# Weight blocks, first queries by halves, the order of the end, and 24 products into an unused bank, in a two-layer gated cross-attention kernel

## The chip, the cores and the metric

The kernel runs on one core of one Trainium2 chip. The metric is the device time of one launch in microseconds (us). The kernel before took 1123.73 us, the median of three runs (1122.61 to 1124.41). Its page and trace come from one profiled execution of 1121.98 us.

A core has five engines, each working through its own queue in order: TensorE (PE; its weight loads are listed apart as PEld), VectorE (DVE), ScalarE (ACT), GpSimd (POOL) and SyncE (SP, which here only issues transfers). An engine waits at an instruction until what it needs has been signalled by another engine or a transfer; everything behind it on that engine waits too.

## What is computed

Four batches `x` of 512 tokens by 512 features go through two layers, each a cross attention and a feed-forward block, both with gates:

```python
x = x + tanh(g_xattn[0]) * L0_xattn(layernorm(x), ctx)      # a WKV recurrence
x = x + tanh(g_ffn[0])   * L0_ffn(layernorm(x), w1, w2, w3)  # 1-bit weights
x = x + tanh(g_xattn[1]) * L1_xattn(layernorm(x), ctx, wq, bq, wkv, bkv, wp, bp)
x = x + tanh(g_ffn[1])   * L1_ffn(layernorm(x), gamma, W)
```

The change touches only layer 1 and its weights:

- `L1_xattn` is attention with 16 heads of 32. The rows of x and of the output, and the weights `wq` and `wp`, are rounded to 8-bit integers: `s = max(absmax(row) / 127, 1e-8)`, `round(x / s)` clipped to ±127, and the products are scaled back by both s.
- `L1_ffn` is one product. Each row is normalised by its root mean square, multiplied by gamma and rounded to 8 bits by its absmax; the weight W is rounded to −1, 0 or 1 after division by its mean absolute value.

## The kernel before, in words

**Tiles.** Batch b lives in `xb`, 128 partitions by 4 row tiles by 512 features; "row t" below is a tile of 128 tokens. A product of depth 512 is four matmuls over blocks of 128. Integer operands are bf16, others f32.

**The order.** Instruction order is laid out by hand. Each stage is a generator, called a line; `place` gives each of its steps a place in time, counted in batches of 17 slots (SLOTS), one slot being about one unit of the attention or of the feed-forward. `run` always advances the line with the lowest place, and the steps' matmuls are chained in the order in which they were emitted (`next_turn`). An `event` is a line of one step (L1332 to L1340). The other engines get what the steps emit; a scheduler keeps each engine's queue near that order. In the boot phase, which lasts until layer 0's feed-forward of batch 0 has ended, places are given by `at_us` or `at_unit`, and there are two PSUM banks with tag m for everything that is not a long sum; later there are three of m, three of hp and two of acc.

**Weights (boot).** `wq`, `wp` and W (keys q, p, f) are loaded as 128x2048 tiles `wn` by `load`. `rounded` (L407) takes the absmax of a whole weight in one DVE reduction (output `w_am`), the scales (`int8_scale`), and then three DVE steps (`quantise`, L253 to L255) for each of four 128x512 blocks into the bf16 `wi` (tag sg, two buffers). For W, `ternary_sums` (L421, output `w_part`) and `ternary` (L430) do the same with one mean. `ints_turned` (L444) transposes the blocks on PE into a bank (`wt_ps`) and DVE copies them (L336) into wqT, wpT or wfT. `output_scales` (L448) transposes wp's scales (`pb_ps`); DVE multiplies them by the gate into `swp_b`. Beside all this run batch 0's feed-forward (`ff_z`, `hr`), the keys and values of the context (`k_half`, V from `v_ps`) and batch 1's WKV recurrence (`wk_q`).

**Attention of layer 1 (`attention_layer`, L855).** `prepared` rounds a row of x and transposes it (`qr_ps`). `project(g)` (L901) makes the queries of four heads for all rows, splits them into two f32r parts (`at_half`) and writes them to memory (`qD`); `fetch_queries` (L939) reads them back, repeated over partitions, as `at_qR`, 4 transfers for a unit (two heads, two rows). SP issues writes and reads in one queue. A unit: `scores` (`s_ps`, maximum on DVE, exponential on ACT), then `turned` (four transposes into `pt_ps`, copied by ACT or DVE), `values` (`o_ps`) and `collect`. There are 16 units a batch, each stage one unit behind the other. The last batch (`alone`) has no feed-forward left beside it; instead batch 2's `ternary_layer` is spread over its units.

**The end.** `project_out` rounds a row of the attention's output, transposes it (`at_oqT`), multiplies it by wpT (`p_ps`) and adds it to x. `statistics` (L1130) gives mean and inverse root of rows; the inverse root is computed by DVE (`rsqrt`, L182: shift, guess, three Newton rounds of three small steps), or by POOL but for its first two steps (`rsqrt_aside`, L199). `ternary` (L1147) makes `tf_xn`, its absmax and scales (`tf_s`, L1162 to L1176), rounds on ACT (L264), transposes (`qr_ps`, ACT's L271 into `tf_xT`), multiplies by wfT (`f_ps`), and DVE's L1189 adds the product to x, which is then stored. For the last batch `end` (L1072) does rows 0 and 1 together, then rows 2 and 3, one step behind the first two; the rsqrt of rows 2 and 3 is POOL's.

Of the kernel before, what the change touches and what calls it, by code (L numbers as in the profile page):

```python
# [30 lines left out]
def kernel(  # L31
# [42 lines left out]
    QSCALE = 1.0 / math.sqrt(DH)  # L74
    GS = 64
    ROWS = 3
    NG = D // GS

    cp = ctx.enter_context(tc.tile_pool(name="const", bufs=1))
# [229 lines left out]
    class Weights:  # L309
# [97 lines left out]
        def rounded(self, key):  # L407
            wn = self.raw.pop(key)
            am = sm.tile([P, NC], F32, name="w_am", tag="w_am")
            absmax(am, wn)  # L410
            s = sq if key == "q" else self.sp
            r = sm.tile([P, NC], F32, name="w_r", tag="w_r")
            int8_scale(s, r, am)
            wi = self.pool.tile([P, NC, D], BF16, name="wi", tag="sg", bufs=2)
            for j in range(NC):
                quantise(wi[:, j, :], wn[:, j, :], r[:, j : j + 1], -127.0)
            self.ints[key] = wi
            if key == "q":
                nc.vector.tensor_scalar(sq, sq, QSCALE, None, ALU.mult)

# [9 lines left out]
        def ternary(self):  # L430
            wn = self.raw.pop("f")
            mf = self.mean_abs(self.fsum, D * D)
            nc.vector.tensor_scalar(mf, mf, 1e-5, None, ALU.add)
            nc.vector.tensor_scalar(
                coef[:, 3:4], mf, gates[:, 3:4], 1.0 / 127.0, ALU.mult, ALU.mult
            )
            rf = cp.tile([P, 1], F32, name="rf")
            nc.vector.reciprocal(rf, mf)
            wi = self.pool.tile([P, NC, D], BF16, name="wi", tag="sg", bufs=2)
            for j in range(NC):  # L440
                quantise(wi[:, j, :], wn[:, j, :], rf, -1.0, 1.0)
            self.ints["f"] = wi

        def ints_turned(self, key):  # L444
            dst = {"q": wqT, "p": wpT, "f": wfT}[key]
# [409 lines left out]
    def attention_layer(b, xb, pool, tiles=range(NT)):  # L855
# [32 lines left out]
            nc.gpsimd.tensor_tensor(xb[:, t, :], xb[:, t, :], bp_b, ALU.add)  # L888
            yield True


        for t in tiles[::2]:
            r = layernorm(xb, tiles=range(t, t + 2))
            yield from in_steps([prepared(t, r), prepared(t + 1, r)], 1)

        qR, kR, V, PT, sums, made, lanes, out_s = {}, {}, {}, {}, {}, {}, {}, {}

        def rows(a):
            return slice(DH * a, DH * (a + 1))

        def project(g):  # L901
            qp = bank("q_ps")[:, 0:n]
            for c in range(NC):
                matmul(
                    qp,
                    lhsT=wqT[:, c, g * P : (g + 1) * P],
                    rhs=xqT[:, c, lo : lo + n],
                    start=(c == 0),
                    stop=(c == NC - 1),
                )  # L910
            q = row("at_q")[:, 0:n]
            nc.vector.scalar_tensor_tensor(
                q, qp, sq[:, g : g + 1], sxb[:, lo : lo + n], ALU.mult, ALU.mult
            )
            half = [row("at_half", F32R)[:, 0:n] for _ in range(2)]
            bias = bqc[:, g : g + 1]
            nc.scalar.activation(half[0], q, AF.Identity, bias=bias)
            nc.vector.scalar_tensor_tensor(
                half[1], q, bias, half[0].bitcast(F32), ALU.add, ALU.subtract
            )  # L920
            for i in range(2):
                nc.sync.dma_start(out=qD[b][g][i, :, lo : lo + n], in_=half[i].bitcast(F32))
# [105 lines left out]
                ALU.mult,  # L1028
            )

        project(0)
        fetch_keys(0)
        fetch_values(0)
        fetch_queries(0)
# [4 lines left out]
        def project_out(t):  # L1039
            s = sm.tile([P, 2], F32, name="at_s", tag="at_s")  # L1040
            o = o_all[:, t, :]
            absmax(s[:, 0:1], o)
            int8_scale(s[:, 0:1], s[:, 1:2], s[:, 0:1])
            rounded(o, s[:, 1:2])
            yield True
            oqT = pool.tile([P, NC, P], BF16, name="at_oqT", tag="at_oqT")
            transposed_rows(oqT, o)
            yield True
            pp = bank("p_ps")
            for c in range(NC):  # L1050
                matmul(
                    pp, lhsT=oqT[:, c, :], rhs=wpT[:, c, :], start=(c == 0), stop=(c == NC - 1)
                )
            if b > NB - 3:
                y = wk.tile([P, D], F32, name="at_y", tag="wk_v")
            else:
                y = row("at_y")
            nc.vector.scalar_tensor_tensor(y, pp, s[:, 0:1], swp_b, ALU.mult, ALU.mult)
            (nc.vector if b > NB - 3 else nc.gpsimd).tensor_tensor(
                xb[:, t, :], xb[:, t, :], y, ALU.add  # L1060
            )
            yield True
# [67 lines left out]
    def statistics(b, xb, tiles):  # L1130

        n = len(tiles)
        mv = sm.tile([P, n, 2], F32, name="mv", tag="mv")
        for i, t in enumerate(tiles):
            s6 = sm.tile([P, 6], F32, name="s6", tag="s6")
            nc.vector.bn_stats(s6, xb[:, t, :])
            nc.vector.bn_aggr(mv[:, i, :], s6)
        v = sm.tile([P, n], F32, name="ln_v", tag="ln_v")
        nc.vector.tensor_scalar(v, mv[:, :, 1], LN_EPS, RMS_EPS, ALU.add, ALU.mult)
        nc.vector.tensor_tensor(v, v, mv[:, :, 1], ALU.add)  # L1140
        y = rsqrt_aside(v, n) if b == NB - 1 and tiles[0] else rsqrt(v, n)
        m = sm.tile([P, n], F32, name="ln_m", tag="ln_m")
        nc.vector.tensor_scalar(m, mv[:, :, 0], -1.0, None, ALU.mult)
        at = {t: slice(i, i + 1) for i, t in enumerate(tiles)}
        return {t: m[:, at[t]] for t in tiles}, {t: y[:, at[t]] for t in tiles}

    def ternary(b, xb, pool, t, r, scale=None):  # L1147


        last = b > NB - 3  # L1150
        if last:

            xn = ff.tile([P, D], F32, name="tf_xn", tag="ff_a", bufs=3)
        else:
            xn = pool.tile([P, D], F32, name="tf_xn", tag="at_row", bufs=ROWS)
        s = sm.tile([P, 3], F32, name="tf_s", tag="tf_s")
        if last:
            nc.vector.scalar_tensor_tensor(
                xn, xb[:, t, :], r[t], gamma_b, ALU.add, ALU.mult
            )  # L1160
            absmax(s[:, 0:1], xn)
            nc.vector.tensor_scalar(s[:, 0:1], s[:, 0:1], scale[t], 1e-5, ALU.mult, ALU.add)  # L1162
        else:
            centred_aside(xn, xb, r, t)
            nc.gpsimd.tensor_tensor(xn, xn, gamma_b, ALU.mult)
            yield True
            absmax(s[:, 0:1], xn)
            nc.vector.tensor_scalar(s[:, 0:1], s[:, 0:1], 1e-5, None, ALU.add)
        nc.vector.reciprocal(s[:, 1:2], s[:, 0:1])
        if last:  # L1170
            nc.vector.tensor_scalar(
                s[:, 1:2], s[:, 1:2], scale[t], 127.0, ALU.mult, ALU.mult
            )
        else:
            nc.vector.tensor_scalar(s[:, 1:2], s[:, 1:2], 127.0, None, ALU.mult)
        nc.vector.tensor_tensor(s[:, 2:3], s[:, 0:1], coef[:, 3:4], ALU.mult)  # L1176
        rounded(xn, s[:, 1:2])
        yield True
        if last:
            xT = ring.tile([P, NC, P], BF16, name="tf_xT", tag="w")  # L1180
        else:
            xT = pool.tile([P, NC, P], BF16, name="tf_xT", tag="at_oqT")
        transposed_rows(xT, xn)
        yield True
        fp = bank("f_ps")
        for c in range(NC):
            matmul(fp, lhsT=xT[:, c, :], rhs=wfT[:, c, :], start=(c == 0), stop=(c == NC - 1))
        xt = xb[:, t, :]
        nc.vector.scalar_tensor_tensor(xt, fp, s[:, 2:3], xt, ALU.mult, ALU.add)  # L1189
        nc.sync.dma_start(out=out[b, t * P : (t + 1) * P, :], in_=xt)  # L1190
        yield True
# [17 lines left out]
    def late(make):  # L1209
        yield from make()  # L1210
# [32 lines left out]
    with (  # L1243
# [88 lines left out]
        for key, w, load in (("q", wq, 11.0), ("p", wp, 12.1), ("f", wf, 13.3)):  # L1332
            event(at_unit(load), lambda key=key, w=w: made.load(key, w))
            if key == "f":
                event(at_unit(load + 0.8), made.ternary_sums)
                event(at_unit(load + 1.2), made.ternary)
            else:
                event(at_unit(load + 1.0), lambda key=key: made.rounded(key))
            line(made.ints_turned(key), (at_unit(load + 1.6), at_unit(load + 2.4), 4))
        event(at_unit(14.7), made.output_scales)  # L1340
        line(
            late(lambda: ffn_layer(xs[0], made)),
            (at_us(67.0), at_us(70.0), 3),
# [18 lines left out]
    for b in range(NB):  # L1362
        if b:
# [9 lines left out]
        line(  # L1373
            late(lambda b=b: attention_layer(b, xs[b], at)),
            (b + 1.0 if b == 0 else b + 0.7, b + 1.03 if b == 0 else b + 0.9, 4),
            (b + 1 + 1.7 / SLOTS, b + 1 + 3.7 / SLOTS, 4),
            (b + 1 + 3.75 / SLOTS, b + 1 + 4.35 / SLOTS, 2),
            (start, end, 72),
# [5 lines left out]
        if b < NB - 1:  # L1384
# [1 line left out]
                late(lambda b=b: ternary_layer(b, xs[b], at)),  # L1386
                (end + 3 / SLOTS, end + 8 / SLOTS, 7)
                if b < NB - 2
                else (end + 4.85 / SLOTS, end + 11.85 / SLOTS, 7),
                aside=b < NB - 2,  # L1390
            )
    run(NB + 9)
# [45 lines left out]
```

## Time and profile before

| | before |
|---|---|
| time, median of 3 runs | 1123.73 us |
| the profiled execution | 1121.98 us |
| its span on the core | 1120.2 us |
| mean granted TensorE clock | 0.954 of full |
| PE busy | 960.3 us (86%) |
| DVE busy | 886.3 us (79%) |
| ACT busy | 711.5 us (64%) |
| POOL busy | 297.8 us (27%) |
| DMA | 189.58 MB, mean 169 GB/s |

The times of the profile count from the start of the span. Busy shares are averages over stages with different limits. Where a line of the profile ends with a bracket, the number in it is the engine's idle time before that line, and the arrow names the engine, the tile and the line of code whose end released it. In the tables of stretches the busy time of each engine stands in us, with the number of instructions, then the granted TensorE clock (1.00 is full, 0.50 half), the share of DMA and its GB/s. A line of the timeline with "x4" joins four instructions of one kind. The boot's stage with layer 1's weights is about 238 to 340 us, the last batch's attention begins about 976, batch 2's last rows lie in 1020 to 1065, and from 1090 only the end of the last batch is left.

### The profile page before, as it was taken

How to read it: one execution, taken by the hardware profiler on the slowest of the kernel's cores; microseconds unless marked ns; L12 is line 12 of the kernel's file. 1: busy time of each engine (PE TensorE's matmuls, PEld its weight loads, DVE VectorE, ACT ScalarE, POOL GpSimd, SP SyncE). 2: the span in 40 equal slices, each digit the busy share in tenths (PEclk: the TensorE clock that was granted, in tenths of full speed). 3: DMA queues.
4: the chain of work that ended last, by engine and by line, in shares of the span. 5: the costliest groups of instructions: out<-in, count | busy, mean ns of one | idle time of the engine just before them, and what ended most of it. 6: DMA issues, size and time to landing. Idle time of an engine off the chain costs nothing.

```text
span 1120.2 us, 16509 instructions
## 1 busy us (share of the span) xinstructions
PE 960.3 (86%) x5520; PEld 678.2 (61%) x5548; DVE 886.3 (79%) x1884; ACT 711.5 (64%) x1454; POOL 297.8 (27%) x301
## 2 busy tenths in 40 slices
PE   3879898978878978899998797999999899788983
PEld 3345565555546756677776475777777677555651
DVE  5887447778877799998759899977689766689866
ACT  5657655453214677667768676687676677887762
POOL 3822014333104143541215536212122400100000
PEclk8889999998888999999999999999999899999997
DMA  8188953544434664654655555464564563243401
GB/s 281 39 274 321 322 203 129 178 169 153 148 122 151 224 191 157 200 178 163 205 188 184 164 168 181 142 220 157 181 227 156 181 201 110 89 134 109 123 11 38
DMA packets 85668, 189.58 MB, mean 169 GB/s; under 512 B 12240, under 2 KB 36816, under 8 KB 74576
## 3 DMA queue, kind: packets, MB, share of 16 engines
q1 hardware_dynamic: 85584, 188.53, 50.2%
q8 instruction: 44, 0.72, 0.3%
q14 instruction: 40, 0.33, 0.1%
HBM read 148.65 MB, written 39.85 MB: 168 GB/s over the span
## 4 chain that ended last, share of the span: by engine, by line
PE 46%; DVE 28%; ACT 12%; issue 5%; DMA 5%; POOL 3%; SPq 1%; POOLq 0%; ACTq 0%; DVEq 0%
PE ff_hp L168 13%; PE ff_acc L168 6%; PE pt_ps L171 6%; PE o_ps L168 4%; PE v_ps L168 3%; PE s_ps L168 3%; DVE wk_q L655 3%; DVE at_nm L962 3%; ACT at_P L964 3%; PE k_ps L168 2%; PE tp_ps L171 2%; DVE qg_i L695 2%; PE qr_ps L171 1%; ACT at_PT L984 1%; DVE ff_z L765 1%
## 5 line engine op out<-in xcount | busy, mean ns | idle before, releaser
L168 PE MATMUL ff_hp<-wT,xp 128*128 128x512 f32 x1024 | 270.5, 408 | 3.3 <-ACT at_P L964 2.1
L168 PEld LDWEIGHTS ff_hp<-wT,xp 128*128 128x128 f32 x1024 | 194.3, 193 | 51.3 <-ACT at_P L964 4.4
L964 ACT ACTIVATE at_P<-s_ps,at_nm 128x512 f32<-128x512 f32 x256 | 174.5, 689 | 61.8 <-DVE at_nm L962 61.4
L962 DVE TENSOR_REDUCE at_nm<-s_ps 128x1 f32<-128x512 f32 x256 | 166.0, 677 | 28.4 <-PE s_ps L168 28.0
L700 POOL TENSOR_TENSOR ff_z<-qg_b,qg_s 128x512 f32<-128x512 bf16 x64 | 71.1, 1111 | 381.1 <-ACT qg_b L699 328.4
L171 PE MATMUL pt_ps<-ident,at_P 128*128 128x128 f32 x1024 | 141.3, 278 | 11.7 <-ACT at_os L1004 5.2
L984 ACT COPY at_PT<-pt_ps 128x512 f32<-128x512 f32 x224 | 124.7, 595 | 38.1 <-PE pt_ps L171 37.5
L171 PEld LDWEIGHTS pt_ps<-ident,at_P 128*128 128x128 f32 x1024 | 113.2, 141 | 53.1 <-issue 13.8
L168 PE MATMUL ff_acc<-wT,hr 128*128 128x512 f32 x512 | 136.6, 408 | 6.3 <-DVE hr L712 3.3
L168 PE MATMUL s_ps<-at_kR,at_qR 128*128 128x512 f32 x256 | 98.1, 449 | 21.9 <-ACT at_P L964 14.6
L168 PEld LDWEIGHTS ff_acc<-wT,hr 128*128 128x128 f32 x512 | 92.4, 190 | 27.3 <-DVE hr L712 4.6
L760 ACT ACTIVATE ff_z<-ff_hp,coef 128x512 f32<-128x512 f32 x64 | 43.9, 686 | 67.2 <-PE ff_hp L168 65.2
L168 PE MATMUL o_ps<-at_PT,at_V 128*32 128x256 f32 x1024 | 72.0, 395 | 1.3 <-DVE hr L712 0.7
L699 ACT CAST qg_b<-qg_i 128x512 bf16<-128x512 int8 x80 | 49.4, 618 | 36.7 <-DVE qg_i L695 24.6
L168 PE MATMUL v_ps<-wkvT,cT 128*128 128x512 f32 x128 | 65.9, 664 | 5.3 <-DVE wT L336 2.3
L765 DVE SCALAR_TENSOR_TENSOR ff_z<-ff_hp,coef,ff_z 128x512 f32<-128x512 f32 x64 | 47.6, 744 | 27.9 <-PE ff_hp L168 27.8
L168 PEld LDWEIGHTS s_ps<-at_kR,at_qR 128*128 128x128 f32 x256 | 45.7, 193 | 39.4 <-ACT at_P L964 23.8
L761 DVE SCALAR_TENSOR_TENSOR ff_z<-ff_z,ff_hp 128x512 f32<-128x512 f32 x64 | 43.4, 679 | 24.2 <-ACT ff_z L760 24.0
L168 PE MATMUL k_ps<-cT,wkvT 128*128 128x512 f32 x128 | 59.3, 613 | 3.1 <-ACT cT L479 1.4
L711 ACT CAST hr<-tp_ps 128x512 fp32r<-128x512 f32 x64 | 37.6, 587 | 35.7 <-PE tp_ps L171 35.7
L655 DVE RECIPROCAL wk_q<-wk_q 128x256 f32<-128x256 f32 x32 | 54.3, 1718 | 1.4 <-POOL wk_p L643 1.4
L171 PE MATMUL tp_ps<-ident,ff_z 128*128 128x128 f32 x256 | 41.2, 286 | 14.4 <-ACT at_PT L984 5.3
(190 smaller groups left out, 1735.7 us busy)
## 6 DMA issues: line engine op xcount, KB each, us to landing
wT<-wD SPq DMA_DIRECT2D x72, 1024.0 KB, 5.2
wn<-in_L_ffn_w_dram SPq DMA_DIRECT2D x18, 1024.0 KB, 6.8
at_kR<-kD SPq DMA_DIRECT2D x128, 128.0 KB, 3.0
at_qR<-qD SPq DMA_DIRECT2D x256, 64.0 KB, 2.2
wD<-wT SPq DMA_DIRECT2D x12, 1024.0 KB, 5.0
kD<-k_half SPq DMA_DIRECT2D x16, 512.0 KB, 3.3
qD<-at_half SPq DMA_DIRECT2D x32, 256.0 KB, 2.1
cn<-in_ctx_dram SPq DMA_DIRECT2D x8, 512.0 KB, 5.9
```

The source lines that it names most:

```text
L168: return in_turn(nc.tensor.matmul(*args, **kwargs))
L171: return in_turn(nc.tensor.transpose(*args))
L655: nc.vector.reciprocal(half, half)
L699: nc.scalar.copy(qb, qi)
L700: nc.gpsimd.tensor_tensor(grouped(src), grouped(qb), s.unsqueeze(2).to_broadcast([P, NG, GS]), ALU.mult)
L711: nc.scalar.copy(part[:, 0, :], pt)
L760: nc.scalar.activation(z, hp, AF.Tanh, scale=coef[:, 0:1])
L761: nc.vector.scalar_tensor_tensor(z, z, 1.0, hp, ALU.add, ALU.mult)
L765: nc.vector.scalar_tensor_tensor(z, hp, coef[:, 1:2], z, ALU.mult, ALU.mult)
L962: nc.vector.tensor_reduce(nm, sp, AX.X, ALU.max, negate=True)
L964: nc.scalar.activation(lanes[k, i, t], sp, AF.Exp, bias=nm, accum_out=sums[k][:, t, i : i + 1],)
L984: made[k] = nc.scalar.copy(dst, blocks(pt))
```

## The change

1. `rounded` and `ternary` become generators: absmax, scales and quantising are done block by block, four steps from 0.8 (q, p) or 1.0 (f) to 1.6 units after the load. For f the sum of magnitudes stays one reduction. `ints_turned` goes from 1.6–2.4 to 1.65–2.45 units after the load, `output_scales` from unit 14.7 to 13.75.
2. In the last batch's attention, `project(0)` is done in two halves: rows 0 and 1 when they are prepared, rows 2 and 3 afterwards. The transfers of the first unit's queries, which are of rows 0 and 1, thus need only the first half.
3. The `ternary_layer` of batch 2 ends at slot 14.65 of the last batch's units, not 11.85.
4. At the end, `rsqrt_aside` is used for rows 0 and 1, not for rows 2 and 3, and the last row's `tf_xn` takes a buffer of another pool (wk_o) in place of one of three in ff_a.
5. After the last row's `p_ps`, PE gets 24 products of a bf16 identity with blocks of wfT, 128x512 each, into a bank of tag m that nothing reads.

```diff
@@ class Weights
         def rounded(self, key):
...
-            absmax(am, wn)
...
-            int8_scale(s, r, am)
-            wi = self.pool.tile([P, NC, D], BF16, name="wi", tag="sg", bufs=2)
+            self.ints[key] = wi = self.pool.tile([P, NC, D], BF16, name="wi", tag="sg", bufs=2)
             for j in range(NC):
-                quantise(wi[:, j, :], wn[:, j, :], r[:, j : j + 1], -127.0)
-            self.ints[key] = wi
+                at = slice(j, j + 1)
+                absmax(am[:, at], wn[:, j, :])
+                int8_scale(s[:, at], r[:, at], am[:, at])
+                quantise(wi[:, j, :], wn[:, j, :], r[:, at], -127.0)
+                yield
...
             for j in range(NC):
                 quantise(wi[:, j, :], wn[:, j, :], rf, -1.0, 1.0)
+                yield
@@ attention_layer
-        def project(g):
+        def project(g, lo=lo, n=n):
...
-        project(0)
+        for t in tiles[::2]:
+            if alone and t:
+                project(0, 0, 2 * P)
+                yield
+            r = layernorm(xb, tiles=range(t, t + 2))
+            yield from in_steps([prepared(t, r), prepared(t + 1, r)], 1)
+
+        if alone:
+            project(0, 2 * P, 2 * P)
+        else:
+            project(0)
...
+            if b == NB - 1 and t == NT - 1:
+                fill = bank("fill_ps")
+                for i in range(WARM):
+                    matmul(fill, lhsT=identb, rhs=wfT[:, i % NC, :], start=True, stop=True)
@@ statistics, ternary
-        y = rsqrt_aside(v, n) if b == NB - 1 and tiles[0] else rsqrt(v, n)
+        y = rsqrt_aside(v, n) if b == NB - 1 and not tiles[0] else rsqrt(v, n)
...
-            xn = ff.tile([P, D], F32, name="tf_xn", tag="ff_a", bufs=3)
+            if t == NT - 1:
+                xn = wk.tile([P, T + 1], F32, name="tf_xn", tag="wk_o")[:, 0:D]
+            else:
+                xn = ff.tile([P, D], F32, name="tf_xn", tag="ff_a", bufs=3)
@@ boot's lines
-                event(at_unit(load + 1.2), made.ternary)
+                line(made.ternary(), (at_unit(load + 1.0), at_unit(load + 1.6), 4))
             else:
-                event(at_unit(load + 1.0), lambda key=key: made.rounded(key))
-            line(made.ints_turned(key), (at_unit(load + 1.6), at_unit(load + 2.4), 4))
-        event(at_unit(14.7), made.output_scales)
+                line(made.rounded(key), (at_unit(load + 0.8), at_unit(load + 1.6), 4))
+            line(late(lambda key=key: made.ints_turned(key)), (at_unit(load + 1.65), at_unit(load + 2.45), 4))
+        event(at_unit(13.75), made.output_scales)
@@ lines of the batches
+            *(() if b < NB - 1 else ((b + 15.8 / SLOTS, b + 15.8 / SLOTS, 1),)),
...
-                else (end + 4.85 / SLOTS, end + 11.85 / SLOTS, 7),
+                else (end + 4.85 / SLOTS, end + 14.65 / SLOTS, 7),
```

More of the change, by code (lines that the diff above doesn't have):

```diff
@@ L76 @@
     ROWS = 3
+    WARM = 24
     NG = D // GS
@@ L438, in ternary @@
             nc.vector.reciprocal(rf, mf)
-            wi = self.pool.tile([P, NC, D], BF16, name="wi", tag="sg", bufs=2)
+            self.ints["f"] = wi = self.pool.tile([P, NC, D], BF16, name="wi", tag="sg", bufs=2)
             for j in range(NC):
                 quantise(wi[:, j, :], wn[:, j, :], rf, -1.0, 1.0)
-            self.ints["f"] = wi
+                yield
         def ints_turned(self, key):
@@ L889, in prepared @@
             yield True
-        for t in tiles[::2]:
-            r = layernorm(xb, tiles=range(t, t + 2))
-            yield from in_steps([prepared(t, r), prepared(t + 1, r)], 1)
         qR, kR, V, PT, sums, made, lanes, out_s = {}, {}, {}, {}, {}, {}, {}, {}
```

## The prediction

> **What bounds the kernel.** I read the page's 40 slices and chain first, then the idle gaps of PE in the timeline around each edit, then tables of busy time by stretches of the clock's length, and last the tail instruction by instruction.
>
> The chain that ended last says who decides:
>
> ```profile
> PE 46%; DVE 28%; ACT 12%; issue 5%; DMA 5%; POOL 3%; SPq 1%; POOLq 0%; ACTq 0%; DVEq 0%
> ```
>
> PE leads, yet over half of the chain lies elsewhere: PE is busy 960.3 of 1120.2 us, and its gaps are short waits for DVE, ACT or a transfer. The change touches four places, about 215 us of span; the rest keeps its order. PE's gaps there (the bracket is idle time and its releaser):
>
> ```profile
> 251.77 0.38 PE L171 MATMUL wt_ps<-identb,sg 128*128 128x128 bf16 x4 [3.63 <-DVE k_half L291]
> 282.15 1.09 PE L171 MATMUL tp_ps<-ident,ff_z 128*128 128x128 f32 x4 [3.54 <-DVE wT L336]
> 318.63 0.58 PE L171 MATMUL wt_ps<-identb,wi 128*128 128x128 bf16 x4 [5.07 <-DVE swp_b L457]
> 980.46 1.19 PE L168 MATMUL s_ps<-at_kR,at_qR 128*128 128x512 f32 x2 [2.35 <-DMA at_qR<-qD]
> 1031.05 0.93 PE L171 MATMUL qr_ps<-ident,tf_xn 128*128 128x128 f32 x4 [2.75 <-ACT tf_xn L264]
> 1104.85 1.97 PE L171 MATMUL qr_ps<-ident,tf_xn 128*128 128x128 f32 x8 [10.62 <-ACT tf_xn L264]
> ```
>
> The first three belong to the weight work, the next to the last batch's first queries, then to batch 2's ternary rows, then to the tail: 27.96 us, the most that could be had. A gap has a second price, in PE's granted clock. These are stretches of 3.41 us laid on the clock's own changes (columns: start:end, length, busy PE, PEld, DVE, ACT, POOL, then the clock):
>
> ```profile
> 1027.88:1031.29 3.41, 0.66 (x7) 0.52 (x6) 3.41 (x13) 2.37 (x6) 0.00 (x0) 1.00 0.76 211
> 1031.29:1034.71 3.42, 3.42 (x23) 1.50 (x22) 3.42 (x14) 2.69 (x6) 0.00 (x0) 0.50 0.06 20
> 1096.15:1099.56 3.41, 0.00 (x0) 0.00 (x0) 3.41 (x11) 0.00 (x0) 0.00 (x0) 1.00 0.00 0
> 1099.56:1102.97 3.41, 0.00 (x0) 0.00 (x0) 3.41 (x17) 0.00 (x0) 0.00 (x0) 0.50 0.00 0
> 1106.39:1109.80 3.41, 1.37 (x5) 0.41 (x5) 2.60 (x10) 2.21 (x4) 0.21 (x2) 0.50 0.00 0
> 1109.80:1113.21 3.41, 3.41 (x12) 1.81 (x11) 1.47 (x2) 0.56 (x1) 0.00 (x0) 0.50 0.21 77
> 1113.21:1116.62 3.41, 2.39 (x12) 1.00 (x11) 1.38 (x3) 1.26 (x2) 0.00 (x0) 1.00 0.20 77
> ```
>
> A stretch with PE busy under about half is followed by one at clock 0.50 (1027.88 → 1031.29), and only a nearly full one brings 1.00 back (1109.80 → 1113.21). At 0.50 the products take 0.449 us each (3.59/8) against 0.2375 (1.90/8).
>
> **Weights block by block.** Removed: two whole-weight absmax (2.29 and 2.27 us), added: eight of about 0.65 (the spacing of other 128x512 DVE steps), so 5.2 − 4.6 = +0.6; plus six more pairs of scale and reciprocal on one column, some 0.07 to 0.2 us each: +0.8 to +2.4. DVE thus works 1.4 to 3 us more. What moves: before 251 the 2.29 absmax stood ahead of k_half, for which PE waited 3.63; behind it now stand blocks of which PE meets one at a time, so I remove 1.5 of that wait, 0.5 near 265, and 1 to 1.5 of the 3.54 at 282. Half of the p blocks then fall into 284 to 300, where DVE idles and has 2.27 us of w_part: that holds V's adds by up to as much as was won. Then the 5.07 at 318.63: there f's twelve quantising steps stand in one run ahead of swp_b (313.40 to 317.84 in DVE's timeline, 4.4 us); spread in four lines, and swp_b asked for earlier (13.75 for 14.7), that wait shrinks by 3 to 4. But a stall of PE freed early meets DVE, busy 86.58 of 102.00 in 238 to 340: something else is late next. Gross about −6.5, of which I give back 4: **−2.5** (ends −5 and +1). Turning is placed 0.05 later, at nothing: PE has the up products beside it, and 0.4 if they aren't there.
>
> **Queries by halves.** at_qR of unit 0 is asked for before the second half of project(0), so the 2.35 us goes. Moved on SP: two qD writes of 128x256, four loads of at_qR ahead of the second half's two writes; unit 1's loads stand behind project(1)'s writes as before, and land about 983.7 where its scores would now be due at 983.3: 0.4 given back. The half-clock stretch 980.09 to 983.51 (PE 3.05 busy) may go with the gap, up to 1.5, but the stretch ahead of it was only 1.42 busy and half of that idle is ACT's and DVE's; I count 0. Added: four more weight loads and products and three small DVE/ACT steps, 0.3 on PE. −2.35 + 0.4 + 0.3: **−1.6** (ends −3 and −0.5). DVE's and ACT's added steps are hidden by the rows being prepared; uncovered they cost 1.
>
> **Batch 2's rows spread.** Each row's steps come about 1.4 units apart, and qr(tf_xn) stands in the middle of a unit instead of at its head, so tf_xn is ready when PE comes. Units here took, o_ps to o_ps, 5.88, 5.45, 9.29, 6.76, 6.19, 6.19, 5.75, 5.84, 5.32 and 5.76 us, 62.43 in all; the rows lie in the third to the eighth. The 9.29 holds the 2.75 wait and a stretch at half clock (1031.29, PE full for 3.42: 1.7 lost). Ten units of 5.4 and four rows of 0.85 for qr and f make 57.4, 5.0 less. PE, 44.49 of 51.10 busy, sets the floor. DVE (43.16) is near its limit too, so I give back 1.5: **−3.5** (ends −5 and −1.5).
>
> **The end and the 24 products.** POOL now takes the rsqrt of rows 0 and 1. Before, POOL took 3.55 us from rs_y to the wait's end:
>
> ```profile
> 1106.72 0.21 DVE L1162 TENSOR_SCALAR tf_s<-tf_s,rs_y 128x1 f32<-128x1 f32 x1 [2.58 <-POOL rs_y L213]
> 1108.86 3.59 PE L168 MATMUL f_ps<-wfT,tf_xT 128*128 128x512 bf16 x8 [2.04 <-ACT tf_xT L271]
> 1115.16 1.61 DVE L1189 SCALAR_TENSOR_TENSOR xb<-f_ps,tf_s,xb 128x512 f32<-128x512 f32 x2 [1.92 <-PE qr_ps L171]
> ```
>
> DVE's rs_y of rows 0, 1 ends at 1097.9; with 3.4 to 3.55 DVE resumes about 1101.3, meanwhile doing two absmax and an xb add, then idling 1.5: a new wait, behind which rows 0, 1's scales and then rows 2, 3's statistics are queued, and ACT's tf_xn waits for the scales. ACT's first tf_xn then starts 1102.0 (was 1104.0), and PE's first turn is at 1102.9 instead of 1104.85. But rows 2 and 3 now take their rsqrt on DVE, and on that in-order engine the two L1189 steps of rows 0, 1, waiting for PE's f_ps, stand inside it. Queued behind them: rows 2, 3's six dependent steps (0.2 each), two scale chains, then ACT's tf_xn, which PE waits for. So ACT starts rows 2, 3's last turn about 1110.1 with PE at full clock and 1111.1 at half, where before it was 1109.55; from there to the last L1189's end before took 7.22 (1116.77 − 1109.55): 1117.3 to 1118.3, and 1115.1 if PE is at full clock throughout. xn's own buffer removes a wait of row 3 for row 0, not the last wait here: nothing.
>
> The 24 products themselves: p_ps ends at 1094.23, 24 × 0.2375 = 5.7, to 1099.9; three us before PE is wanted, hence nothing on PE while the clock is full; at half clock 10.8, to 1105, +1.7 at most. Do they hold the clock? Two idle gaps remain: 2.9 us from 1099.9 to 1102.9, and some 4.8 between rows 0, 1 and rows 2, 3. The Trainium skill ("TensorE: Matmul & The Clock Gate", HAM oscillation — how this bites in real kernels) says: no PE idle longer than about 3.4 us. By it rows 0, 1 run warm, rows 2, 3 cold: 1117.3. By the rows above, a stretch needs only be half idle, and 2.9 idle of 3.41 is that for most positions of the stretches: rows 0, 1 are cold as well, 1118.3. The measured rows decide; but a stretch can straddle the gap, so 1117.6: **+0.8** (ends −1.6, +1.7).
>
> **Sum.** −2.5 − 1.6 − 3.5 + 0.8 = −6.8 on 1121.98 (span 1120.2 and 1.8 around it): 1115.2. The profiled run lay 1.75 under the median of 1123.73, so against the median 1117.0. All low ends: −14.6; all high: +0.7; independent, some ±4.
>
> **Rivals.** *Won time isn't kept (0.22).* The three body parts each free PE, and DVE, 79% busy over the span, becomes the bound: boot 0, queries −1, rows −1.5, tail +0.8: −1.7, 1122.0. For it: DVE's 86.58 of 102. Against: PE was at least as busy beside it in the rows' stage. *The fill holds the clock (0.12).* Pair 2 starts warm too: tail −1.6 instead of +0.8: 1114.6. Against: 4.8 us of idle, which neither rule forgives. *The change doesn't do what it says (in 0.5, the likeliest).* The fill leaves the clock as it was and pair 1's lead is lost on DVE; body gains alone carry it: 1117.0. *Slower (0.08).* One mechanism: blocks of weights, emitted in DVE's order as runs of absmax, scale, reciprocal and three quantising steps (0.65 + 0.4 + 1.3 = 2.35 us), each stand ahead of a DVE step that empties one of PE's two m banks in the boot. PE has some 1 us of work ahead; eight q and p blocks cost it 1.35 each, 10.8, while the old gaps of about 2.5 go: boot +8.3; with the others −4.3: +4.0, 1127.7. It decides from about +4.3 on the boot. For it: today's waits on k_half and wT are just that. Against: DVE idles 15 us there. *More than hoped (0.08):* low ends of all, about 1112.
>
> **Numbers.** A measurement here tells 0.2% (2.2 us) from no change. Faster 0.8, within 0.12, slower 0.08: half of the kept-time rival lies within. Range 1112.5 to 1122.0.
>
> **What would show it.** Right: no PE gap over 1.5 us at unit 0's scores; no 2.75 us gap and no 0.50 stretch near 1031; the wait near 318 below 2.5; clock 0.50 for rows 2, 3; the tail from p_ps's end to the last L1189 about 23 us (before 22.5). Wrong: a new DVE wait over 3 us in 284 to 318; rows 2, 3 at full clock; units of batch 2 still near 6.4 us.

## The result, and the profile after

The changed kernel took 1123.28 us, the median of 14 runs (1120.23 to 1128.23); the kernel before, run beside it, 1122.72 (1118.96 to 1125.04). The ratio is 1.0015, with a 95% interval of 1.0000 to 1.0029: no gain, perhaps a loss of up to 0.3%. I had forecast 1117.0, 0.6% faster. The profiled execution took 1124.38 us, its span 1122.6, PE was busy 971.4 us and the mean clock 0.954, as before.

The gaps of PE that answer to those shown of before (timeline of PE, the changed kernel; in brackets the idle time and its releaser):

```profile
249.97 0.38 PE L172 MATMUL wt_ps<-identb,sg 128*128 128x128 bf16 x4 [2.92 <-DVE k_half L292]
277.69 0.63 PE L172 MATMUL tp_ps<-ident,ff_z 128*128 128x128 f32 x4 [2.79 <-DVE wT L337]
...
298.79 0.23 PE L172 MATMUL wt_ps<-identb,wi 128*128 128x128 bf16 x1 [1.96 <-DVE wi L256]
300.77 0.29 PE L172 MATMUL wt_ps<-identb,wi 128*128 128x128 bf16 x1 [1.75 <-DVE wi L256]
...
317.07 0.23 PE L172 MATMUL wt_ps<-identb,wi 128*128 128x128 bf16 x1 [1.10 <-DVE wi L256]
319.13 0.23 PE L172 MATMUL wt_ps<-identb,wi 128*128 128x128 bf16 x1 [1.83 <-DVE wi L256]
320.39 0.23 PE L172 MATMUL wt_ps<-identb,wi 128*128 128x128 bf16 x1 [1.03 <-DVE wi L256]
...
986.93 0.70 PE L169 MATMUL s_ps<-at_kR,at_qR 128*128 128x512 f32 x2 [0.97 <-DMA at_qR<-qD]
991.25 0.50 PE L169 MATMUL s_ps<-at_kR,at_qR 128*128 128x512 f32 x1 [2.51 <-ACT at_P L961]
...
1105.36 1.82 PE L172 MATMUL qr_ps<-ident,tf_xn 128*128 128x128 f32 x8 [4.01 <-ACT tf_xn L265]
1113.40 1.97 PE L172 MATMUL qr_ps<-ident,tf_xn 128*128 128x128 f32 x8 [3.43 <-ACT tf_xn L265]
```

The old waits are gone or smaller: 5.07 for swp_b, 2.35 for the first queries, 2.75 for tf_xn. In the weights' stage there are five new ones of another kind (the last five lines with `wi`): PE waits at a transpose of `wi` until DVE has written that very block. They come to 7.67 us. At 991 a new wait of 2.51 us stands where unit 1 of the attention begins.

To see where the time went I matched DVE's and ACT's steps of the two traces (the n-th step of a tile with the n-th) and took the difference of their times. The weights' stage is measured between the same two ff_z steps of ACT: 136.80 us before, 138.54 after, +1.74. From the queries' stage to about 1000 us it is −0.8, in the rows' stage to 1075 us −1.8. The end, from the start of the last row's first p_ps to the end of the last add, is 23.57 before and 24.54 after, +0.97.

What is left of the 2.4 us between these two profiles comes from code that the change doesn't touch, mostly between 360 and 930 us; it is taken up last.

### The profile page after: what moved, and what is told of

It is laid out like the page before. It is cut to its first block, busy times and chain, and to the rows that moved or that the text cites. A ratio compares the mean times of both kernels' runs of the same rounds, so it can differ in the third digit from the quotient of the medians.

```text
span 1122.6 us, 16585 instructions
## 1 busy us (share of the span) xinstructions
PE 971.4 (87%) x5548; PEld 684.5 (61%) x5576; DVE 887.6 (79%) x1904; ACT 711.4 (63%) x1455; POOL 297.8 (27%) x301
## 4 chain that ended last, share of the span: by engine, by line
PE 47%; DVE 27%; ACT 13%; DMA 5%; issue 4%; POOL 3%; SPq 0%; ACTq 0%; POOLq 0%; DVEq 0%
PE ff_hp L169 14%; PE pt_ps L172 6%; PE ff_acc L169 6%; PE o_ps L169 4%; PE s_ps L169 4%; ACT at_P L961 3%; PE v_ps L169 3%; DVE wk_q L657 3%; DVE at_nm L959 2%; DVE qg_i L697 2%; PE k_ps L169 2%; ACT at_PT L981 2%; PE tp_ps L172 2%; PE qr_ps L172 1%; DVE qg_s L250 1%
## 5 line engine op out<-in xcount | busy, mean ns | idle before, releaser
L169 PE MATMUL ff_hp<-wT,xp 128*128 128x512 f32 x1024 | 275.4, 413 | 3.3 <-ACT at_P L961 2.1
L169 PEld LDWEIGHTS ff_hp<-wT,xp 128*128 128x128 f32 x1024 | 197.4, 196 | 52.5 <-ACT at_P L961 4.4
L169 PEld LDWEIGHTS ff_acc<-wT,hr 128*128 128x128 f32 x512 | 93.9, 193 | 27.1 <-DVE hr L714 5.0
L961 ACT ACTIVATION_READ_ACCUMULATOR at_P<-s_ps,at_nm 128x1 f32 x256 | 52.4, 205 | 0.0
```

What stands on the lines that cost most here:

```text
L169: return in_turn(nc.tensor.matmul(*args, **kwargs))
L961: nc.scalar.activation(lanes[k, i, t], sp, AF.Exp, bias=nm, accum_out=sums[k][:, t, i : i + 1],)
```

## The experiments

All were compared with runs of the kernel before on the same chip; the interval is that of the ratio. "Weights' stage" is the stretch named above in the run's one profile, "PE idle" the part of it in which PE did nothing (its length less PE's busy time), "end" the stretch from the start of the last row's first p_ps.

| run | median us (before beside it) | ratio, 95% interval | weights' stage | PE idle | end |
|---|---|---|---|---|---|
| before, the profile shown | | | 136.80 | 25.6 | 23.57 |
| the change | 1123.28 (1122.72) | 1.0015, 1.0000–1.0029 | 138.54 | 27.0 | 24.54 |
| e1_boot | 1124.78 (1123.36) | 1.0013, 1.0000–1.0025 | 136.93 | 27.2 | 22.52 |
| e2_noboot | 1119.78 (1123.36) | 0.9982, 0.9967–0.9997 | 135.70 | 26.5 | 23.45 |
| e3_lateturn | 1112.71 (1123.36) | 0.9909, 0.9884–0.9935 | 127.69 | 21.3 | 24.31 |
| e4_nofill | 1123.18 (1123.36) | 1.0007, 0.9991–1.0023 | 136.77 | 27.1 | 24.73 |
| f1_scalesearly | 1122.33 (1122.42) | 0.9998, 0.9984–1.0012 | 135.49 | 25.7 | 22.53 |
| f2_bootlate | 1114.32 (1122.42) | 0.9923, 0.9904–0.9942 | 125.76 | 22.3 | 22.55 |
| f3_oldend | 1111.78 (1122.42) | 0.9901, 0.9878–0.9924 | 126.85 | 21.6 | 24.39 |
| f4_hold | 1111.95 (1122.42) | 0.9899, 0.9881–0.9916 | 124.42 | 21.2 | 22.28 |
| g1_best | 1111.89 (1123.01) | 0.9907, 0.9879–0.9935 | 124.41 | 21.1 | 23.59 |
| g2_besthold | 1107.76 (1123.01) | 0.9863, 0.9834–0.9893 | 126.29 | 21.2 | 21.22 |
| g3_plate | 1122.10 (1123.01) | 0.9993, 0.9978–1.0008 | 135.67 | 25.6 | 24.60 |
| e6_qr | 1120.41 (1123.01) | 0.9978, 0.9962–0.9993 | 133.99 | 26.3 | 23.72 |
| h1_flate | 1119.17 (1123.67) | 0.9950, 0.9932–0.9968 | 132.34 | 24.1 | 24.58 |
| h2_pflate | 1119.52 (1123.67) | 0.9963, 0.9945–0.9981 | 135.55 | 24.6 | 24.54 |

**e1_boot**: before with the change's part 1 alone (`rounded`, `ternary` and their lines).

> The kernel before with the weights block by block alone. Theory (the turned blocks wait): PE gains about 4 us up to 290 us, as far as wq, and loses it again where wp's and W's turning stands in PE's order before their last blocks are quantised; at 360 us it is 1 to 2 us later than before, and the time is before + 1.5. Rival (the boot gained as forecast, and the loss is elsewhere): at 360 us it is 2.5 us earlier, time before - 2.5.

The ratio fits the theory (+1.4 us), the rival's −2.5 lies outside the interval. The stage has the same waits on wi as the changed kernel: 1.97, 1.75, 1.10, 1.83, 1.04.

**e2_noboot**: the changed kernel with part 1 taken back.

> The changed kernel with the weights as before; queries by halves, spread rows, the end and the 24 products stay. Theory: queries -0.8, rows -1.8, end +1 to +2, sum about -1: 1 us under before and 1.7 under the changed kernel. Rival (the boot is harmless): it takes as long as the changed kernel or longer, 1123 to 1126.

3.6 us under before in the medians, 2.0 by the ratio; −0.8 and −1.8 in the two stages again. Its interval lies wholly under that of the change: the loss is in the boot.

**e3_lateturn**: the changed kernel, with one line moved.

```diff
-            line(late(lambda key=key: made.ints_turned(key)), (at_unit(load + 1.65), at_unit(load + 2.45), 4))
+            line(late(lambda key=key: made.ints_turned(key)), (at_unit(load + 1.95), at_unit(load + 2.75), 4))
```

> The changed kernel with the turning of wq, wp and W placed 0.3 units later (load + 1.95 to 2.75). Theory: the waits of PE for wi near 298, 301 and 317 to 320 us (7.7 us together) go or fall below 2.5 together, the gain of 4 us at 290 is kept for the most part: at 360 us 2 to 3 us earlier than before, time 3 to 4 us under the changed kernel. Rival (VectorE is the bound there): another wait of the same sum comes, time within 1 us of the changed kernel.

Far more than expected: 10.6 us under before, the stage 10.85 us shorter than the changed kernel's. All that this line moves is the place of PE's transposes, and of DVE's and ACT's copies of them: they now stand behind a further sum or two of the feed-forward. What stays of the waits over 0.9 us between 279 and 325 us (PE's timeline of this run; the only one for `wi` is 1.80):

```profile
279.80 5.14 PE L169 MATMUL v_ps<-wkvT,cT 128*128 128x512 f32 x8 [2.44 <-DVE wT L337]
...
301.73 0.23 PE L172 MATMUL wt_ps<-identb,wi 128*128 128x128 bf16 x1 [1.80 <-DVE wi L256]
302.99 0.41 PE L172 MATMUL wt_ps<-identb,wi 128*128 128x128 bf16 x4 [1.02 <-DVE xb L670]
324.64 0.38 PE L172 MATMUL wt_ps<-identb,wi 128*128 128x128 bf16 x4 [1.15 <-DVE wfT L337]
```

**e4_nofill**: the changed kernel without part 5.

> The changed kernel without the 24 products. Theory (they hold nothing that counts): rows 0, 1 turn at half clock (1.97 us for eight), rows 2, 3 as in the changed kernel; VectorE sets both starts, so the last step moves by under 0.5 us and the time by less than can be told. Rival (they hold the clock): the end takes 1.5 to 3 us longer without them.

As expected: 1123.18 against 1123.28. The first turn of rows 0, 1 starts 10.17 us behind the start of that p_ps without the products and 10.22 with them, the end is 24.73 and 24.54.

**f1_scalesearly**: before, with `output_scales` at 13.75 in place of 14.7 and nothing else.

> The kernel before with output_scales alone moved from unit 14.7 to 13.75; weights in one piece as before. Theory (blocks and a later turning are both needed): the 5.07 us wait for swp_b goes, but the next step of PE that needs VectorE meets the same run of 12 quantising steps, so less than 1.5 us is won at 360 us and the time is within 1.5 us of before. Rival (the earlier scales are the whole gain of the later turning): 4 us or more earlier at 360 us.

The 5.07 wait goes, two waits of 2.39 and 1.57 for W's `wi` take its place at 316 and 318, and the time is before's. Taking that one wait away wins nothing measurable, because PE meets the rest of the same run of quantising steps at its next transposes.

**f2_bootlate**: before with part 1 and e3's line.

> The kernel before with the weights block by block and their turning 0.3 units later, nothing else. Theory: at 360 us 7 to 9 us earlier than before; time before - 7, 8 us under the block by block kernel with the turning as placed by the change. Rival (it needed the other parts): under 3 us.

8.1 us under before: it needs none of the other parts.

**f3_oldend** and **g1_best**: e3 with the inverse roots as before and no added products; g1 also has the last row's old buffer.

> The changed kernel with the later turning, but the inverse roots at the end as before (VectorE for rows 0, 1, POOL for rows 2, 3) and without the 24 products. Theory (the new order of the end costs 1 us): from the last row's first p_ps to the last step 22.5 to 23.6 us where the later turning alone has 24.3; time 0.5 to 1.5 under it, 1111.5. Rival (the end gained): 1 us longer.

> Blocks with the later turning, queries by halves and the spread rows; the end, the last row's buffer among it, as before, no added products. Theory (in the run with the old inverse roots it was the last row's own buffer that let its step and its absmax go ahead of the scales of rows 0, 1 on VectorE): from the last row's first p_ps to the last step 22.5 to 23.6 us, 1 to 1.5 less than in that run; ScalarE's first rounding of rows 0, 1 10.3 to 10.8 us behind that p_ps, not 11.5. Time 1110.5. Rival (that run's end was slow by its clock alone): the rounding stays at 11.5.

f3 missed: its end is as long as e3's, 24.39. ACT's first rounding of rows 0, 1 came 11.54 us behind p_ps, where before has 10.78. g1 has 10.78 again and an end of 23.59. In f3's trace DVE does the last row's tf_xn step (1092.04) ahead of the scales of rows 0, 1 (1092.70), in g1's the scales come first. So the last row's own buffer, which I had at nothing, lets that step pass them; with the old roots this costs 0.8 between the two profiles. The two times don't tell it (1111.78 and 1111.89).

**f4_hold**: e3, with 38 products, and 14 more into a bank behind row 1's f_ps.

> The changed kernel with the later turning, 38 products in place of 24, and 14 more behind the product of row 1, so that PE idles less than 1 us ahead of either pair. Theory (24 end too early, and a stretch that is half idle takes the clock): the clock stays 1.00 to the last product, rows 2, 3 take 4.1 us from their first turn to the last step where they took 6.3, the end is 1.3 to 2.2 us shorter. Rival (VectorE alone sets the end, or more products stand in the way): the end as long as with 24, or longer.

The end, in PE's timeline of this run:

```profile
1085.05 8.36 PE L169 MATMUL fill_ps<-wfT,identb 128*128 128x512 bf16 x38
1094.41 1.36 PE L172 MATMUL qr_ps<-ident,tf_xn 128*128 128x128 f32 x8 [1.00 <-ACT tf_xn L265]
1095.85 1.90 PE L169 MATMUL f_ps<-wfT,tf_xT 128*128 128x512 bf16 x8
1097.58 3.19 PE L169 MATMUL fill_ps<-wfT,identb 128*128 128x512 bf16 x14
1102.34 1.36 PE L172 MATMUL qr_ps<-ident,tf_xn 128*128 128x128 f32 x8 [1.57 <-ACT tf_xn L265]
1103.78 1.90 PE L169 MATMUL f_ps<-wfT,tf_xT 128*128 128x512 bf16 x8
```

No stretch at half clock up to the last product: eight turns take 1.36 instead of 1.97, eight products 1.90 instead of 3.59. From the first turn of rows 2, 3 to the last add it is 4.13 us (expected 4.1), the end 2.03 shorter than e3's. In the time of the whole kernel this is inside the noise (1111.95 and 1112.71).

**g2_besthold**: g1 with 44 products behind the last p_ps.

> The run before it in this list with 44 products behind the last p_ps, which last to about 10.8 us behind that p_ps's start. Theory (the clock stays full up to rows 0, 1, and VectorE and POOL set the starts of rows 2, 3): end 0 to 0.5 us shorter than without, about 22.2 us, time 1110. Rival (the products delay rows 0, 1, or the clock sets the end): 1 us longer, or more than 1 us shorter.

The best version: 1107.76, 1.4% under before (interval 1.1 to 1.7). The expectation missed the end by 1 us, and its rival came true: 21.22, 2.4 shorter than g1's, so there the clock did set it (g1 is at half clock from 1083.58 to 1100.65, from 3 us behind the start of its end to shortly before its last products; g2 is at full clock to the last product). The medians lie 4.1 us apart, but with six executions each the two intervals overlap. With DVE's roots for rows 0, 1 and POOL's for rows 2, 3 the second pair follows the first so closely that no second filling is needed.

**g3_plate, h1_flate, h2_pflate**: the changed kernel with the turning of wp, of W, and of both 0.3 units later.

> The changed kernel with the turning of wp alone 0.3 units later. Theory (each turning waits for its own blocks): the two waits near 298 and 301 (3.7 us) go, those of W near 317 to 320 (4.0 us) stay; 3 to 5 us earlier at 360 us than the changed kernel, time 1119 to 1120. Rival (one of the two alone is the cause, the other's wait is only moved): 0 or 9 us and more.

> The changed kernel with the turning of W alone 0.3 units later. Theory (each turning waits for its own blocks, and the three add up): W's waits near 317 to 320 us (4.0) fall below 1.5, those of wp near 298 and 301 stay; 3 to 4 us earlier at 360 us than the changed kernel, time 1120. Rival (W's turning is nearly the whole loss): 8 us or more, time 1114.

> The changed kernel with the turning of wp and W 0.3 units later, that of wq as in the change. Theory (they add up, and wq's has its part): 6 to 8 us earlier at 360 us than the changed kernel, time 1116. Rival (wq's place doesn't matter): as with all three later, 10 to 12 us, time 1112 to 1113.

wp's alone takes 2.87 us out of the stage, W's alone 6.20, both together only 2.99, all three 10.85. The expectations of g3 and h2 missed: in these profiles the parts don't add. Most of that is the clock. PE's idle time falls by 1.4 (wp), 2.9 (W), 2.4 (both) and 5.7 us (all three), but PE is busy 110.97 us in h2 and 108.25 in h1 for the same 458 products, because h2's stage has 30.7 us at half clock and h1's 23.9:

```profile
224.65:356.99 132.34, 108.25 (x458) 71.90 (x457) 110.77 (x275) 48.80 (x83) 35.25 (x34) 0.91 0.45 155
223.34:358.89 135.55, 110.97 (x458) 74.50 (x457) 111.67 (x275) 49.16 (x82) 35.24 (x34) 0.89 0.44 151
```

(h1, then h2). In whole times, where many executions are averaged, the ratios put the three 2.5, 7.3 and 5.8 us under the changed kernel, each known to some 2.5 us, so that 5.8 against the sum of 9.8 is hardly out of the noise. "Each waits for its own blocks" is still too simple: in g3 and h2 the waits for wp's `wi` go, and PE waits 2.39 us near 299 for DVE's add of V instead. In all three wq's turning still stands ahead of v_ps, as in the change. What its place is worth isn't shown: v_ps's eight products before 287 take 6.76 us in the changed kernel and 5.14 in e3, where wq's turning stands behind them, but 5.24 in g3 and h1.

**e6_qr**: before with parts 2 and 3.

> The kernel before with the first queries by halves and batch 2's spread rows, nothing else. Theory: -0.8 to -1.1 between 940 and 1010 us and -1.8 between 1010 and 1075 us, the rest as before; time before - 2.7. Rival (they gain what was forecast): -5.

2.6 us under before, 2.5 by the ratio (interval 0.8 to 4.3): the theory, and not −5.

## Why the prediction was wrong, point by point

**Weights: wrong, and this is the failed step.** The prediction said: "Turning is placed 0.05 later, at nothing: PE has the up products beside it". I costed DVE's added steps and the waits removed, and never asked whether each turning's blocks would be there when PE, in its own order, came to it. Before, a weight was quantised in one piece at 1.0 units behind the load (W at 1.2) and turned from 1.6; now its last block is asked for at 1.4 (W's at 1.45), and the turning stands at 1.65: 0.25 units behind it where there had been 0.6. All four columns of the transposed weight need all four blocks of rows, so PE waits for the last block at the first column. And that block is late, because DVE's queue has other steps between (DVE's timeline of the changed kernel; PE's two transposes at 298.79 and 300.77 start as these two `wi` steps end):

```profile
296.13 2.27 DVE L429 TENSOR_REDUCE w_part<-wn 128x64 f32<-128x2048 f32 x1
298.32 0.41 DVE L256 TENSOR_SCALAR wi<-wn 128x512 bf16<-128x512 f32 x1
...
300.28 0.43 DVE L256 TENSOR_SCALAR wi<-wn 128x512 bf16<-128x512 f32 x1
```

I had named w_part in just that place and let it hold V's adds; it held wp's last blocks, and PE with them. Up to 294 us the forecast held: the stage ran 3.5 us ahead of before, and at 305 it was 3.1 behind. The slower rival had the right place and a wrong mechanism: it let each block hold a DVE step that empties one of PE's banks, but the waits for k_half and wT shrank (2.92 and 2.79), and the new waits are for the blocks themselves.

The sum of the waits says what happened. The three old ones gave up 0.71 + 0.75 + 5.07 = 6.53 us, which is the gross −6.5 that I had, by luck: at the first I had 1.5 and at the last 3 to 4. The five new ones, which the prediction had at nothing, take 7.67: a loss of 1.1 (smaller changes, such as 1.02 us at 279.34 for wqT, are left out).

How large is it, by the kernels that share the weights' code? In PE's idle time without the change 25.6, 26.5 and 26.3 (before, e2, e6), with it 27.0, 27.2 and 27.1 (the change, e1, e4): +1.0, about the balance of the waits. With the later turning it is 21.1 to 22.3 in six runs. In the length of the stage: without the change 136.80, 135.70, 133.99, mean 135.5; with it 138.54, 136.93, 136.77, mean 137.4: +1.9 against my −2.5. With the later turning 124.41 to 127.69, mean 125.9: −9.6. Of the +1.9, the 0.9 us beyond the idle time is PE's busy time, and that goes with the clock: it lies between 107.7 and 111.2 us in the three without the change, so the 0.9 isn't shown to belong to the change. The stage in three kernels (columns as in the tables of stretches):

```profile
224.34:361.14 136.80, 111.22 (x458) 74.05 (x457) 110.35 (x257) 48.83 (x83) 35.22 (x34) 0.89 0.44 149
```

before; the change:

```profile
223.76:362.30 138.54, 111.56 (x458) 73.70 (x457) 112.00 (x275) 48.76 (x83) 34.69 (x34) 0.90 0.45 147
```

and the later turning:

```profile
224.42:352.11 127.69, 106.38 (x458) 70.88 (x457) 110.66 (x275) 48.50 (x83) 35.02 (x34) 0.93 0.47 158
```

DVE is busy 1.65 us more with the change, in the 1.4 to 3 that I had. PE's idle time (length less busy) is 25.6, 27.0 and 21.3: of the 10.85 between the last two, 5.7 is idle time and 5.2 is PE itself, the same 458 products done at a better clock. So a wait was paid twice, as I had written of the gaps, but for its own sum I hadn't used it. DVE, with 110.66 of 127.69 us, was not the bound that I took it for when I gave 4 us back. The rival of the time that isn't kept was nearest in number (1122.0), but it too had DVE as the bound, and the later turning wins with DVE nearly as busy as in the change (112.00).

**Queries by halves: right mechanism, half the size.** −0.8 in the two profiles, about −0.7 between kernels that share the code (without f2, whose stage met two stretches at half clock), against −1.6. Part of it is the clock: the stretch at half clock at 980, for which I had counted 0, is gone in the changed kernel; in e3 and g1, which have one at 982 and 978, the gain is only 0.4 and 0.5. At unit 0's scores the gain is 3.2; unit 1 gives 2.3 back. Its transfer costs 0.97 (I had 0.4), and the 2.51 wait behind that is a chain I had not seen: the late scores meet DVE in the middle of batch 2's absmax steps, so its maxima come at 989.54, ACT's exponential at 990.44, and PE waits for a bank.

**Spread rows: right mechanism, half the size.** The ten units took 62.43 us before and 60.63 after, −1.8 against −3.5; in four kernels with the old rows 62.43 to 62.55, in twelve with the spread ones 60.60 to 60.64. The 2.75 wait and the half-clock stretch at 1031 went. But 57.4 for the ten was too good, and so was 58.9 after giving back 1.5: in the prediction's own measure, from one unit's first o_ps to the next, the ten now take 4.88 to 7.07 us, on average 6.06, where I had 5.4 without and 6.25 with a row. Why they don't get down to 5.4 wasn't looked into.

**The end: size and steps right, one term not separated.** +0.97 against +0.8 in the profiles; the six with the end before take 22.52 to 23.72 (mean 23.1), the six with the change's end and the 24 products 23.45 to 24.60 (mean 24.3). Rows 2, 3 run at half clock and DVE works without a pause from 1103.80 to 1112.69, as I had it. The 24 products took 5.34 us, not 5.7, and rows 0, 1 came half a us later than I had, so the gap behind the products was 4.01, not 2.9. What the new order of the roots costs alone isn't shown: with the old roots and the last row's own buffer the end is 24.39 (f3), as long as with both new (e3, 24.31), and no run has the new roots with the old buffer. "xn's own buffer … nothing" was wrong at least beside the old roots. The clock fell as the rows' rule says (the changed kernel, stretches laid on the clock's own; the first number behind the length is PE's busy time, the clock stands third from the end):

```profile
1102.36:1105.78 3.42, 0.42 (x4) 0.42 (x4) 1.98 (x11) 1.29 (x2) 0.99 (x6) 1.00 0.00 0
1105.78:1109.19 3.41, 3.19 (x12) 1.63 (x11) 3.38 (x15) 1.60 (x3) 0.00 (x0) 0.50 0.02 5
1109.19:1112.60 3.41, 0.77 (x4) 0.16 (x2) 3.18 (x18) 0.07 (x1) 0.00 (x0) 1.00 0.41 154
1112.60:1116.02 3.42, 2.62 (x10) 1.85 (x11) 0.09 (x2) 2.75 (x4) 0.00 (x0) 0.50 0.00 0
```

With a gap of 4.01 the Trainium skill's rule ("TensorE: Matmul & The Clock Gate", HAM oscillation — how this bites in real kernels) says the same, so this run doesn't part the two; the gap of 2.75 us in the kernel before, behind which the clock fell at 1031.29, does, and there the measured rows decide. That the change doesn't do what it says held: 24 products end too early, e4_nofill shows it, and f4_hold and g2_besthold show that enough of them do it.

**Sum.** +1.9 − 0.7 − 1.9 + 1.2 = +0.5 us, against +0.56 in the medians and +1.7 by the ratio (interval 0.0 to 3.3), so that the fit to a tenth is luck. Of the 7.3 us between this and my −6.8, 4.4 lie in the weights, 1.6 in the rows, 0.9 in the queries and 0.4 in the end.

**The signs.** All five signs that I had named for "right" came true (no wait over 1.5 us at unit 0's scores, no 2.75 us gap and no half clock near 1031, 1.83 us near 318, half clock for rows 2, 3, 23.5 us from p_ps's end to the last add), none of those for "wrong", and yet the sum was wrong. They looked at the old waits; the new ones were five of under 2 us each, below the 3 us that I had set as a sign.

**Open.** That the later turning works by PE's order is shown: in e3 the waits for `wi` fall from 7.67 to 1.80 us and PE's idle time by 5.7. Why the three turnings don't quite add up in that idle time (1.4 and 2.9 against 2.4 together), and which neighbour in PE's order matters most, wasn't settled.

## What to carry to other kernels

When a producer is cut into pieces, look at the consumer in the other engine's fixed order: if each of its steps needs all the pieces, it must keep its distance from the last piece, not from the first. An estimate that lists the removed waits should list, for every moved step, when its last operand is ready and when its engine gets there. Products that hold the clock must reach up to the work that they are to warm, and be counted in time, not in number.

## What was not expected of the hardware

The clock's stretches lie where they like against the work, and this alone moves the time. Two of the 64 ff_z steps of ACT bound a stretch from about 360 to 922 us, in which PE has the same products in all of them (the traces of f1, f2, f3 and f4 have records of 19 that the others lack). Yet it took 561.50 us before, 561.53 in e2_noboot, 565.34 in e1_boot and 567.90 in g2_besthold. Two of them:

```profile
360.45:921.95 561.50, 507.96 (x3150) 386.45 (x3167) 473.05 (x1015) 394.09 (x833) 180.48 (x169) 0.98 0.55 184
```

before, and g2_besthold (whose profiled execution, 1113.64 us, was the slowest of its six):

```profile
349.64:917.54 567.90, 515.89 (x3150) 392.42 (x3167) 473.66 (x1015) 394.02 (x834) 180.87 (x169) 0.97 0.55 181
```

PE is busy 7.93 us more with the same 3150 products. The place of the clock's 3.413 us grid against the first of these steps, read from the changes of clock in each of the sixteen traces:

| grid behind the first step, us | length, us | stretches at half clock |
|---|---|---|
| 0.06 (the change), 0.36 (f2) | 563.93, 565.14 | 10, 10 |
| 0.77 (g2) | 567.90 | 11 |
| 1.29 (e6), 1.56 (g3), 1.58 (e1), 1.60 (e4), 1.70 (h1) | 565.04, 565.29, 565.34, 565.24, 565.50 | 10 each |
| 1.82 (before), 1.82 (e2) | 561.50, 561.53 | 6, 6 |
| 1.96 (f1) | 565.74 | 10 |
| 2.96 (f4) | 566.69 | 11 |
| 2.99 (e3), 2.99 (g1) | 564.34, 564.53 | 8, 8 |
| 3.03 (h2), 3.04 (f3) | 563.49, 563.52 | 9, 9 |

Kernels within 0.02 us of each other's place agree within 0.2 us, whatever else differs in them; a few hundredths more can decide over several stretches (2.96, 2.99 and 3.03).

Whether a gap of PE brings the next stretch to half clock depends on where it falls in the grid. Laid on that grid from 60 us on, the sixteen traces bear out the prediction's rule with blurred edges: behind a stretch at full clock in which PE was busy under 0.40 of the time, half clock always followed (184 times); over 0.60 it never did (4114 times); between, both occur. Back to full clock is possible from a busy share of 0.77 on, not only from a nearly full stretch as the prediction had it. (PE's ends are modelled in the profile and some of its records are missing, so these shares are rough.)

Between 360 and 922 us the place of the grid makes up to 6.4 us, more than any part of this change was worth, so one profile against one other does not measure a change of this size, and the profile of before that I read was at the best place of the sixteen.
